# Selective-scan block: roots and fp8 casts moved to ScalarE, nine instead of six products with C of each chunk moved to GpSimd

## The chip, the cores and the metric

The kernel runs on one core of one Trainium2 chip. The metric is device time in microseconds (us), the median over runs. Engines are named as in the profile: PE is TensorE (PEld its weight loads), DVE is VectorE, ACT is ScalarE, POOL is GpSimd, SP is SyncE, which here only issues DMAs. Each engine runs its own instructions in the order in which the program wrote them; engines wait for one another through semaphores.

## The reference

The input is x of shape (8, 96, 64, 64) in float32: 8 images, 96 channels, 4096 positions. Layer 0 is a selective scan, layer 1 a linear attention and a quantised two-layer network.

```python
u = groupnorm(x) as tokens;  xm, z = u @ in_proj_w.T          # 192 channels each
xm = silu(conv1d(xm, 4 taps));  dt, Bm, Cm = xm @ x_proj_w.T   # 6, 16, 16
delta = softplus(dt @ dt_proj_w.T + dt_proj_b);  A = -exp(A_log)
h[t] = exp(delta * A) * h[t-1] + delta * Bm * xm               # 16 states per channel
y = sum over states of h * Cm, + D * xm;  y = y * silu(z)
x = x + layernorm(y @ out_proj_w.T)
t = t + attention(layernorm(t))                                # linear: (q k^T) v, no softmax
t = t + ffn(layernorm(t))       # operands rounded to fp8 (5,2), sums to fp16, relu between
```

## The kernel before

**Tiling.** Images go in pairs (p, 4 of them) and positions in chunks of T = 512 (c, 8 of them), so there are 32 chunks, worked one after another. A chunk's scan has 192 channels x 16 states x 2 images = 6144 rows. A *unit* is two tiles of 128 rows x 512 positions, and a chunk has NU = 24 units: j (3 groups of 64 channels) x g (4 groups of 4 states) x b (2 halves of the states). Unit u has j = u // 8, g = (u // 2) % 4, b = u % 2.

**A unit** (`unit`, L711) has these operations.
- `products_b` (L656): POOL multiplies du (delta times xm, spread over the states) by a row of B, which gives dbu. It runs AHEAD = 3 units early, into four buffers.
- `decay` (L675): ACT computes exp(delta A) into a PSUM tile da, once for each half h; there are two da buffers, so the decay of the next unit starts when this unit's scan of the same half has ended.
- The scan (L741): DVE computes hs from da and dbu, two instructions of 512 positions. hs has three buffers.
- The product with C: in most units PE first makes a tile cc in PSUM by a selection matmul (`rows_c`, L664), and DVE multiplies hs by cc (L763), giving pr. In the units listed in POOLED, POOL does it instead (`pooled`, L767) at the start of the next unit, from a tile c that a broadcast DMA has filled with rows of C (`rows`, L639).
- `sums` (L688): PE adds the pr tiles of a pair of units over their states into the PSUM tile y. `gate` (L707) on DVE multiplies the finished y of a group j by silu(z).
- A small copy on ACT (L719) keeps the last state of the unit for the next chunk.

**Everything else** is written as generators that are advanced between units by a table, STEPS (L37): the text before the bar is run ahead of the scans of a unit, that behind it after them. P (`chain_p`) prepares the chunk after the next: group norm, convolution, Silu, B, C, delta with Softplus. E (`chain_e`) does the output projection, layer norm and residual of the chunk before, and the norm of the attention. W builds the attention matrices of an image pair. F0 and F1 (`chain_f`) do attention and the two-layer network of a chunk that lies LAG = 9 back, one for each image; they start with chunk 9, and those of the last nine chunks make up the tail of the program. G collects group-norm statistics of the next pair.

**What sets the order.** The program is written under a manual schedule: instructions stand on each engine in program order. `later` (L381) puts a few jobs on lists that `now` empties at fixed places of a unit: "norms" at its start, "others" after its scans; `settle` empties one early if its result is needed. At unit SILU = 10 two decays of unit 12 are written early into other PSUM banks, since Silu's long block on ACT follows.

**Norms.** `norm_stats` (L399) has DVE collect mean and variance, then on POOL: minus the mean (L412), add eps (L131), the root by a power of -0.5 (L132), and the product that gives the shift (L414). `normalise` (L418) is an ACT instruction with that scale and shift. A chunk has two norms of E (8 columns) and, from chunk 9 on, two of F (4 columns).

**Casts.** In F, `rounded` copies a matmul result to fp16 on ACT (L997), `relu` applies bias and relu (on ACT in the chunks, L1007; on DVE in the tail, L1003), and a job on "others" has POOL cast it to fp8 (L1011). The second matmul (L1033) needs the three casts.

**Tables.** ACT needs an activation table for Silu, one for Softplus and one for Exp; a load (ACT_TABLE_LOAD) stands in front of the first instruction that needs a table not in place.

Of the kernel before, what the change touches and what calls it, by code (L numbers as in the profile page):

```python
# [8 lines left out]
F32 = mybir.dt.float32  # L9
F32R = mybir.dt.float32r  # L10
F16 = mybir.dt.float16
# [4 lines left out]
C = 96  # L16
NS = 16
NJ = 3
NG = 4
# [5 lines left out]
POOLED = (4, 5, 12, 13, 20, 21)  # L25
POOLED_G = 2
SILU = 10
ROWS_B = (16, 18, 20, 22)
AHEAD = 3

# [10 lines left out]
    3: "F1 F0 P | F1 G6",  # L41
    4: "| E",
# [23 lines left out]
def tile_mamba_linear_attention_ffn(  # L66
# [60 lines left out]
    nc.vector.memset(mhalf, -0.5)  # L127

# [102 lines left out]
    def passing(shape, name):  # L231
        t = p2.tile([128, 2, T], F32, tag="pr", name=name, bufs=4)
        return view(t, shape)
# [165 lines left out]
    def norm_stats(src, n, tag):  # L399

        mv = p2.tile([128, n, 2], F32, tag=f"mv{tag}", name="mv")
        rstd = p2.tile([128, n], F32, tag=f"rs{tag}", name="rs")
        nmr = p2.tile([128, n], F32, tag=f"nm{tag}", name="nm")
        st = p1.tile([128, n, 6], F32, tag=f"st{tag}", name="st")
        for i in range(n):
            nc.vector.bn_stats(st[:, i, :], src[:, i, :])  # L406
        for i in range(n):
            nc.vector.bn_aggr(mv[:, i, :], st[:, i, :])


        def ends():
            nc.gpsimd.tensor_scalar_mul(nmr, mv[:, :, 0], -1.0)  # L412
            rsqrt(rstd, mv[:, :, 1], 1e-5)
            nc.gpsimd.tensor_mul(nmr, nmr, rstd)  # L414

        return rstd, nmr, later("norms", ends)

    def normalise(dst, src, norm, q):  # L418
        settle(norm[2])
        nc.scalar.activation(  # L420
            dst, src, AF.Identity, bias=norm[1][:, q : q + 1], scale=norm[0][:, q : q + 1]
        )
# [4 lines left out]
    def load_x(p, c):  # L427

        t = p1.tile([C, 2, T + 3], F32, tag="x", name="x")
        h = 3 if c else 0  # L430
        if not c:
            nc.gpsimd.memset(t[:, :, 0:3], 0.0)
        nc.sync.dma_start(
            t[:, :, 3 - h : T + 3],
            x[2 * p : 2 * p + 2, :, c * T - h : (c + 1) * T].rearrange("b c t -> c b t"),
        )
        x_next[p, c] = t

    def chain_p(p, c, s, after):
# [53 lines left out]
        nc.scalar.activation(zs, zs, AF.Silu)  # L493
        yield
# [26 lines left out]
        nc.scalar.activation(delta, delta, AF.Softplus)  # L521
        yield
# [18 lines left out]
    def first_p(s, after):  # L541
# [75 lines left out]

        cs = s["cs"] = p2.tile([128, T], F32R, tag="cs", name="cs")
# [3 lines left out]
        rows(s, "c", 2 * NS, POOLED_G)  # L622
# [16 lines left out]
    def rows(s, to, of, g):  # L639

        t = s[to, g] = p2.tile([128, 2, T], F32, tag=to, name=to, bufs=NG if to == "b" else 1)
        for n in range(NG):
            nc.sync.dma_start(
                t[32 * n : 32 * n + 32],
                s["bd"][of : of + 2 * NS].rearrange("(b n) t -> n b t", b=2)[NG * g + n]
                .unsqueeze(0)
                .to_broadcast([32, 2, T]),
            )

    def rows_b(s, g):  # L650
        rows(s, "b", 0, g)
# [12 lines left out]
    def rows_c(s, u):  # L664
        j, g, b = where(u)
        if u in POOLED:
            return
        if ("low", 0) in s:
            settle(s["low", 0])
        cc = s["cc", u] = ps_all.tile([128, T], F32, tag="cc", name="cc", bufs=2)  # L670
        nc.tensor.matmul(  # L671
            cc, lhsT=sel[64:128, g, b], rhs=s["cs"][64:128, :], start=True, stop=True
        )
# [37 lines left out]
    def unit(s, prev, nxt, first, u, steps):  # L711
# [4 lines left out]
        if u - 1 in POOLED:  # L716
            pooled(s, u - 1)
# [10 lines left out]
        if u - 3 in POOLED and u % 2 == 0:  # L728
            sums(s, u - 3)
        if u % 2 == 0 and (u or prev is not None) and (u - 1) not in POOLED:  # L730
            sums(s if u else prev, (u or NU) - 1)
# [3 lines left out]
        if to is not None:  # L735
            products_b(to, v)
        hs = s["hs", u] = p2.tile([128, 2, T], F32, tag="hs", name="hs", bufs=3)
# [22 lines left out]
        if u in POOLED:  # L760
            return
        pr = s["pr", u] = p2.tile([128, 2, T], F32, tag="pr", name="pr", bufs=4)
# [4 lines left out]
    def pooled(s, u):  # L767
        j, g, b = where(u)
        pr = s["pr", u] = p2.tile([128, 2, T], F32, tag="pq", name="pr")
        nc.gpsimd.tensor_mul(  # L770
            pr, s["hs", u], s["c", g][:, b, :].unsqueeze(1).to_broadcast([128, 2, T])
        )
# [165 lines left out]
    def chain_f(p, c, b, banks, lane=None):  # L938
# [5 lines left out]
        def place(tag, out_tag, bufs):  # L944
# [5 lines left out]
            [128, NK, C], F32, name="x2", **place(f"x2{b}", ("pr", "b")[(lane or 0) % 2], 4)  # L950
# [34 lines left out]
        casts = []  # L985
# [13 lines left out]
        def relu(m):  # L999
# [6 lines left out]
            else:  # L1006
                nc.scalar.activation(h16[m], h16[m], AF.Relu, bias=b1q[:, m : m + 1])  # L1007
            casts.append(
                later(
                    "others",  # L1010
                    lambda: nc.gpsimd.tensor_copy(h8[0][:, m, :], h16[m], saturate=False),  # L1011
                )
            )
# [15 lines left out]
        for job in casts:  # L1029
            settle(job)  # L1030
# [6 lines left out]
        y16 = p2.tile([C, T], F16, name="y16", **place("y16", "pq", 2))  # L1037
# [73 lines left out]
    waiting.update(norms=[], others=[])  # L1111
    with tc.manual_schedule():
# [5 lines left out]
        for i, (p, c) in enumerate(chunks):  # L1118
# [4 lines left out]
            def steps(u, part):  # L1123
                if part == 0:
# [6 lines left out]
                    if nxt is not None and u == NU - 1:  # L1131
                        rows(nxt, "c", 2 * NS, POOLED_G)
# [9 lines left out]
    s = slots[N - 1]  # L1142
    sums(s, NU - 1)
# [83 lines left out]
```

## Time and profile before

| | us |
|---|---|
| median of 3 runs (3163.77 to 3164.42) | 3163.89 |
| span of the profiled execution | 3160.5 |
| first scan starts, last scan pair starts | 69.5, 3005.7 |
| busy: PE, DVE, ACT, POOL | 2469.6, 2935.2, 2263.9, 2840.7 |
| one chunk, median of the time between the first scans: chunks 0 to 8, 9 to 30 | 87.5, 93.9 |

The profile is of one execution. A row of the groups reads: line, engine, operation, output <- inputs, shapes, count | busy us, mean ns of one | idle time of the engine just before such instructions and what ended it. A row of the waits reads: who waited <- for whom: us in total, times, the longest. A row of the order of time reads: start, duration, engine, line, operation, count, and in brackets the idle time before it. A row of the stretches has, after the window and its length, the busy us and the count of instructions of each engine in it. Matmul ends are modelled, so PE's busy time is no measure of its peak. "Idle before" matters only on the engine that sets the pace.

### The profile page before, as it was taken

Reading aid. Unit: us, or ns where it says so; the run is one execution under the profiler, and the core shown is the slowest. Engines: PE = TensorE matmul, PEld = TensorE weight load, DVE = VectorE, ACT = ScalarE, POOL = GpSimd, SP = SyncE. Lnnn points to the kernel's source line nnn. Section 1 sums busy time; section 2 is a strip of 40 time slices with the busy share of each in tenths; the row PEclk is TensorE's granted clock in tenths of the full one; section 3 lists DMA queues with packets and bytes.
Section 4 is the critical chain, followed back from the end, with each engine's and each line's share of the span. In section 5 each row is a group of like instructions: output and inputs, shape, how many; then the busy total and the mean of one; then the engine's idle time right before and its main releaser. Section 6 shows DMA issues by size and latency. Waiting matters only on the chain. (4 is left out here: it accounts for less than half of the span.)

```text
span 3160.5 us, 35127 instructions
## 1 busy us (share of the span) xinstructions
PE 2469.6 (78%) x9450; PEld 928.7 (29%) x9450; DVE 2935.2 (93%) x4265; ACT 2263.9 (72%) x4360; POOL 2840.7 (90%) x1921
## 2 busy tenths in 40 slices
PE   6787787878787777777777778777888778887777
PEld 2122222222222223222233323222323222332344
DVE  4999999999999999999999999999999999999945
ACT  3666666667677777777777777777877777777656
POOL 2999999999999999999999999999999999999955
PEclk8677777787778888888888877898888888877668
DMA  6655556665555667555667555567565466755322
GB/s 149 152 122 137 134 156 152 160 150 135 141 143 135 138 162 175 146 129 125 141 164 170 141 146 125 137 157 170 146 148 127 124 144 162 169 132 134 95 70 73
DMA packets 253037, 443.75 MB, mean 140 GB/s; under 512 B 37605, under 2 KB 45990, under 8 KB 252838
## 3 DMA queue, kind: packets, MB, share of 16 engines
q1 hardware_dynamic: 247846, 439.40, 56.9%
q10 hardware_dynamic: 4992, 2.11, 0.3%
q8 instruction: 74, 1.21, 0.2%
q14 instruction: 125, 1.02, 0.1%
HBM read 349.11 MB, written 92.27 MB: 140 GB/s over the span
## 5 line engine op out<-in xcount | busy, mean ns | idle before, releaser
L659 POOL TENSOR_TENSOR dbu<-du,b 128x1024 f32<-128x1024 f32 x768 | 1804.6, 2371 | 112.6 <-DVE hs L741 65.5
L741 DVE TENSOR_TENSOR_SCAN hs<-da,state,dbu 128x512 f32<-128x512 f32 x1290 | 1573.5, 1265 | 25.6 <-ACT da L681 24.6
L681 ACT ACTIVATE da<-dl,aneg 128x512 f32<-128x512 f32 x1474 | 1000.6, 688 | 665.4 <-DVE hs L741 644.2
L763 DVE TENSOR_TENSOR pr<-hs,cc 128x1024 f32<-128x1024 f32 x576 | 698.7, 1213 | 35.1 <-DVE hs L741 0.5
L695 PE MATMUL y<-pr,ssum 128*32 128x512 f32 x2816 | 585.1, 831 | 113.3 <-DVE pr L763 113.3
L770 POOL TENSOR_TENSOR pr<-hs,c 128x1024 f32<-128x1024 f32 x192 | 453.8, 2363 | 36.6 <-DVE hs L741 30.4
L459 PE MATMUL mp<-u,wk 96*64 96x512 f32 x1488 | 398.1, 658 | 66.6 <-ACT xm L477 66.4
L671 PE MATMUL cc<-cs,sel 64*128 64x512 f32 x576 | 330.0, 583 | 144.8 <-DVE pr L763 144.4
L671 PEld LDWEIGHTS cc<-cs,sel 64*128 64x128 f32 x576 | 121.6, 215 | 557.3 <-DVE pr L763 296.8
L741 DVE TENSOR_TENSOR_SCAN hs<-da,dbu 128x512 f32<-128x512 f32 x184 | 213.2, 1205 | 17.4 <-POOL dbu L659 9.9
L516 PE MATMUL mp<-dbl,dtT 12*128 12x512 f32 x186 | 158.9, 947 | 56.8 <-ACT cs L506 38.5
L695 PEld LDWEIGHTS y<-pr,ssum 128*32 128x32 f32 x2816 | 87.9, 132 | 380.6 <-DVE pr L763 201.6
L791 PE MATMUL mE<-woT,zs 128*128 128x192 f32 x744 | 146.6, 350 | 66.7 <-ACT t1e L799 45.1
L459 PEld LDWEIGHTS mp<-u,wk 96*64 96x64 f32 x1488 | 97.0, 145 | 293.6 <-issue 156.6
L132 POOL TENSOR_TENSOR rs<-rs,mhalf 128x8 f32<-128x8 f32 (+1 forms) x128 | 173.3, 1354 | 10.7
L791 PEld LDWEIGHTS mE<-woT,zs 128*128 128x128 f32 x744 | 127.3, 200 | 126.8 <-ACT t1e L799 70.5
L703 PE MATMUL y<-xm,dd 128*128 128x512 f32 x192 | 129.2, 760 | 22.4 <-DVE zs L709 21.9
L467 PE MATMUL mp<-u,wz 96*64 96x512 f32 x372 | 137.0, 825 | 4.3 <-ACT xm L485 4.3
L1011 POOL CAST h<-h 128x512 fp8e5<-128x512 f16 x192 | 117.6, 622 | 24.8 <-DVE h L1003 15.8
L719 ACT COPY state<-hs 128x2 f32<-128x2 f32 x736 | 130.1, 181 | 0.2
L420 ACT ACTIVATE o<-x,nm,rs 128x96 f32<-128x96 f32 x256 | 98.6, 455 | 36.4 <-POOL nm L414 34.4
L531 POOL TENSOR_TENSOR du<-delta,xm 128x512 f32<-128x512 f32 x93 | 117.1, 1273 | 0.0
(306 smaller groups left out, 3234.1 us busy)
## 6 DMA issues: line engine op xcount, KB each, us to landing
du<-lu SPq DMA_DIRECT2D x380, 256.0 KB, 5.5
dl<-ld SPq DMA_DIRECT2D x380, 256.0 KB, 7.9
b<-bd SPq DMA_DIRECT2D x512, 128.0 KB, 5.0
lu<-du SPq DMA_DIRECT2D x96, 256.0 KB, 5.7
ld<-delta SPq DMA_DIRECT2D x93, 256.0 KB, 2.4
c<-bd SPq DMA_DIRECT2D x128, 128.0 KB, 4.4
xg<-in_x_dram SPq DMA_DIRECT2D x32, 384.0 KB, 3.8
xr<-in_x_dram SPq DMA_DIRECT2D x32, 384.0 KB, 8.7
```

The lines of the kernel that those rows point to most:

```text
L132: nc.gpsimd.tensor_tensor(out_, out_, mhalf[0 : out_.shape[0], 0 : out_.shape[1]], op=ALU.pow)
L459: nc.tensor.matmul(ps[64 * b : 64 * b + 64, :], lhsT=wk[:, k, 64 * j : 64 * j + 64], rhs=u[:, b, k : k + T], start=(k == 0), stop=(k == 3),)
L467: nc.tensor.matmul(ps[64 * b : 64 * b + 64, :], lhsT=wz[:, 64 * j : 64 * j + 64], rhs=u[:, b, 3 : T + 3], start=True, stop=True,)
L516: nc.tensor.matmul(ps, lhsT=dtT[:, j, :], rhs=dbl[0 : 2 * RANK, :], start=True, stop=True)
L659: nc.gpsimd.tensor_mul(dbu, s["du", j][:, 2 * b : 2 * b + 2, :], s["b", g][:, b, :].unsqueeze(1).to_broadcast([128, 2, T]),)
L671: nc.tensor.matmul(cc, lhsT=sel[64:128, g, b], rhs=s["cs"][64:128, :], start=True, stop=True)
L681: nc.scalar.activation(da, s["dl", j][:, 2 * b + h, :], AF.Exp, scale=aneg[:, 2 * j + h, g : g + 1])
L695: nc.tensor.matmul(s["y"][q : q + 32, :], lhsT=ssum, rhs=pr[:, h, :], start=False, stop=(g == NG - 1),)
L741: nc.vector.tensor_tensor_scan(hs[:, h, :], s.pop(("da", u, h)), dbu[:, h, :], 0.0 if first else state["last"][:, u, h : h + 1], ALU.mult, ...
L763: nc.vector.tensor_mul(pr, hs, s.pop(("cc", u)).unsqueeze(1).to_broadcast([128, 2, T]))
L770: nc.gpsimd.tensor_mul(pr, s["hs", u], s["c", g][:, b, :].unsqueeze(1).to_broadcast([128, 2, T]))
L791: nc.tensor.matmul(ps[:, 2 * k * C : 2 * (k + 1) * C], lhsT=zs[:, j, tok : tok + 128], rhs=woT[:, j].rearrange("p b c -> p (b c)"), start= ...
```

## The change

Six things, in one edit.
- POOLED becomes 0, 2 and 5 of every eight units (nine in a chunk instead of six), and those products are issued as before at the start of the next unit.
- Their rows of C come in three tiles of 128 x 512 (c0, c1, c2), each loaded by four broadcast DMAs, in units 20 and 22 of the chunk before and in unit 1, instead of one tile of 128 x 1024 loaded in unit 23.
- All products share one rotation of PRB = 5 buffers (before: four for DVE's and two for POOL's). The sums of the pairs (0,1) and (2,3) of eight move to units 3 and 5, those of (4,5) and (6,7) to the next unit 0.
- The root is now Ln (with eps as bias) and Exp (scale -0.5) on ACT, and a negation there; POOL keeps one product per norm, written behind `products_b` of the unit. Group norm keeps the old root.
- In the chunks, the fp8 cast runs on ACT directly behind the relu. In the tail it stays on POOL.
- After Silu and after Softplus the table with Exp and Ln is loaded explicitly. One F0 step moves from unit 3 to unit 4.

```diff
-POOLED = (4, 5, 12, 13, 20, 21)
-POOLED_G = 2
+POOLED = (0, 2, 5)
+ROWS_POOLED = {20: (0, 0), 22: (1, 0), 1: (2, 1)}
+PRB = 5
-    3: "F1 F0 P | F1 G6",
-    4: "| E",
+    3: "F1 P | F1 G6",
+    4: "| F0 E",
...
-        def ends():
-            nc.gpsimd.tensor_scalar_mul(nmr, mv[:, :, 0], -1.0)
-            rsqrt(rstd, mv[:, :, 1], 1e-5)
-            nc.gpsimd.tensor_mul(nmr, nmr, rstd)
-        return rstd, nmr, later("norms", ends)
+        def power():
+            nc.scalar.activation(rstd, mv[:, :, 1], AF.Ln, bias=eps5)
+            nc.scalar.activation(rstd, rstd, AF.Exp, scale=-0.5)
+            nc.scalar.mul(nmr, rstd, -1.0)
+        def shift():
+            nc.gpsimd.tensor_mul(nmr, nmr, mv[:, :, 0])
+        return rstd, nmr, (later("norms", power), later("shifts", shift))
...
+    def exp_and_ln():
+        nc.scalar.preload_act_table_set("natural_log_exp_and_others")
...
         nc.scalar.activation(zs, zs, AF.Silu)
+        exp_and_ln()
...
         nc.scalar.activation(delta, delta, AF.Softplus)
+        exp_and_ln()
...
+    def rows_pooled(s, g, b):
+        t = s["c", g, b] = p2.tile([128, T], F32, tag=f"c{g}", name="c", bufs=1)
+        for n in range(NG):
+            row = 2 * NS + NS * b + NG * g + n
+            nc.sync.dma_start(
+                t[32 * n : 32 * n + 32], s["bd"][row : row + 1].to_broadcast([32, T])
+            )
...
-        if u - 1 in POOLED:
+        if u and (u - 1) % 8 in POOLED:
             pooled(s, u - 1)
...
-        if u - 3 in POOLED and u % 2 == 0:
-            sums(s, u - 3)
-        if u % 2 == 0 and (u or prev is not None) and (u - 1) not in POOLED:
-            sums(s if u else prev, (u or NU) - 1)
+        if u % 8 == 0 and (u or prev is not None):
+            of, v = (s, u) if u else (prev, NU)
+            sums(of, v - 3)
+            sums(of, v - 1)
+        if u % 8 in (3, 5):
+            sums(s, u - 2)
         now("norms")
         steps(u, 0)
...
             products_b(to, v)
+        now("shifts")
...
-        pr = s["pr", u] = p2.tile([128, 2, T], F32, tag="pq", name="pr")
+        pr = s["pr", u] = p2.tile([128, 2, T], F32, tag="pr", name="pr", bufs=PRB)
...
-            casts.append(
-                later("others",
-                    lambda: nc.gpsimd.tensor_copy(h8[0][:, m, :], h16[m], saturate=False)))
+            if after:
+                nc.gpsimd.tensor_copy(h8[0][:, m, :], h16[m], saturate=False)
+            else:
+                nc.scalar.activation(h8[0][:, m, :], h16[m], AF.Copy, saturate=False)
...
-                    if nxt is not None and u == NU - 1:
-                        rows(nxt, "c", 2 * NS, POOLED_G)
+                    if u in ROWS_POOLED:
+                        to = s if u < NU // 2 else nxt
+                        if to is not None:
+                            rows_pooled(to, *ROWS_POOLED[u])
```

## The prediction

> **What bounds the kernel now.** I read the busy shares first, then the stretches of time, then the groups of instructions, then the chain of waits, and last the order of time in one chunk.
>
> ```profile
> PE 2469.6 (78%) x9450; PEld 928.7 (29%) x9450; DVE 2935.2 (93%) x4265; ACT 2263.9 (72%) x4360; POOL 2840.7 (90%) x1921
> ```
> ```profile
> core 0: us, PE busy (x) PEld busy (x) DVE busy (x) ACT busy (x) POOL busy (x), PEclk, DMA share, GB/s
> 69.00:856.00 787.00, 620.51 (x2159) 202.83 (x2159) 766.66 (x935) 526.62 (x985) 727.70 (x393) 0.76 0.60 143
> 856.00:2918.00 2062.00, 1628.77 (x6418) 609.91 (x6418) 1977.94 (x2818) 1569.59 (x3015) 1934.89 (x1277) 0.83 0.60 146
> 3005.00:3160.50 155.50, 116.46 (x518) 74.20 (x518) 80.03 (x314) 93.45 (x206) 85.52 (x164) 0.74 0.23 72
> ```
>
> The first stretch is chunks 0 to 8, the second chunks 9 to 30 (with F work), the third the tail. In the first two DVE is busy 97% and 96% of the time: DVE sets the pace, POOL is close behind (92%, 94%), ACT has room (67%, 76%). Per chunk that is 87.4 us with DVE 85.2 and POOL 80.9 in the first stretch, and 93.7 us with DVE 89.9, POOL 87.9 and ACT 71.3 in the second.
>
> ```profile
> L741 DVE TENSOR_TENSOR_SCAN hs<-da,state,dbu 128x512 f32<-128x512 f32 x1290 | 1573.5, 1265 | 25.6 <-ACT da L681 24.6
> L763 DVE TENSOR_TENSOR pr<-hs,cc 128x1024 f32<-128x1024 f32 x576 | 698.7, 1213 | 35.1 <-DVE hs L741 0.5
> L770 POOL TENSOR_TENSOR pr<-hs,c 128x1024 f32<-128x1024 f32 x192 | 453.8, 2363 | 36.6 <-DVE hs L741 30.4 <-DMA xr<-in_x_dram 3.6 <-DMA xg<-in_x_dram 1.4
> L1011 POOL CAST h<-h 128x512 fp8e5<-128x512 f16 x192 | 117.6, 622 | 24.8 <-DVE h L1003 15.8 <-ACT h L1007 2.1 <-PE cc L859 1.8
> L132 POOL TENSOR_TENSOR rs<-rs,mhalf 128x8 f32<-128x8 f32 x64 | 106.8, 1670 | 5.3
> L132 POOL TENSOR_TENSOR rs<-rs,mhalf 128x4 f32<-128x4 f32 x64 | 66.5, 1039 | 5.3
> L997 ACT CAST h<-mF 128x512 f16<-128x512 f32 x147 | 85.0, 578 | 10.2 <-POOL h L1011 6.7 <-PE mF L989 3.1
> L1007 ACT ACTIVATE h<-h,b1q 128x512 f16<-128x512 f16 x138 | 97.0, 720 | 0.0
> L719 ACT COPY state<-hs 128x2 f32<-128x2 f32 x736 | 130.1, 181 | 0.2
> ```
>
> These are the prices: a product with C costs 1.213 on DVE and 2.363 on POOL, a root 1.670 or 1.039, a cast 0.622 on POOL.
>
> ```profile
> ACT da L681 <- DVE hs L741: 644.2, 820, 4.0
> DVE hs L741 <- ACT da L681: 31.7, 43, 1.2
> ```
>
> ACT mostly waits for DVE's scans (644.2 us); DVE waits 31.7 us for ACT's decays. Where, the order of time shows: units 12 to 14 of chunk 15, DVE and then ACT.
>
> ```profile
> 1468.46 2.46 DVE L741 TENSOR_TENSOR_SCAN hs<-da,state,dbu 128x512 f32<-128x512 f32 x2 [1.00 <-ACT da L681]
> 1471.59 2.46 DVE L741 TENSOR_TENSOR_SCAN hs<-da,state,dbu 128x512 f32<-128x512 f32 x2 [0.67 <-ACT da L681]
> ```
> ```profile
> 1462.04 1.28 ACT L492 ACT_TABLE_LOAD   x1
> 1463.34 1.48 ACT L492 ACTIVATE xm<-xm 128x1536 f32<-128x1536 f32 x1
> 1464.73 1.47 ACT L493 ACTIVATE zs<-zs 128x1536 f32<-128x1536 f32 x1
> 1466.10 0.27 ACT L719 COPY state<-hs 128x2 f32<-128x2 f32 x2
> 1466.38 1.28 ACT L681 ACT_TABLE_LOAD   x1
> 1467.67 1.30 ACT L681 ACTIVATE da<-dl,aneg 128x512 f32<-128x512 f32 x2
> ```
>
> Silu's block delays the decay for unit 13 by 1.00 us, and the F copies behind it delay unit 14 by 0.67 us.
>
> **Part by part.**
>
> *Products with C.* Units 0, 2, 5 of eight instead of 4, 5, 12, 13, 20, 21: 288 on POOL instead of 192. DVE loses 96 x 1.213 = 116.4 us (3.64 per chunk), POOL gains 96 x 2.363 = 226.9 (7.09 per chunk). On DVE this lies on the path. PE drops 96 selection matmuls; PE is not on the path.
>
> *Roots.* POOL loses 128 roots with the add and the negation (L131, L412, 0.231 to 0.257 each in the groups): 64 x (1.670 + 0.248 + 0.257) + 64 x (1.039 + 0.231 + 0.255) = 236.8 us. ACT gains three small instructions per norm. The trace shows no Ln; the nearest row is the 0.181 us state copy, the far end POOL's 0.257 for 128x8: 128 x 3 x 0.181 = 70 us, at most 99. I take 70, the same engine's row. Ln now waits on ACT for DVE's statistics; behind it stand the next unit's decays, which wait for a scan that DVE runs after these statistics anyway: nothing. Without that cover it would cost 0.54 per norm. The shift stays on POOL (0.204), now behind the dbu product; in unit 17 it waits for ACT's Softplus block, by my count some 2 us, and POOL is 4 us early for the next buffer it has to free. The normalisations wait for this shift; they stand a unit later or behind the decays (F0's moved from unit 3 to 4): nothing.
>
> *Casts.* POOL loses 138 x 0.622 = 85.8 us, ACT gains 138 of 0.578 (PSUM copy) to 0.720 (relu on the same SBUF tile). I take 0.63, between two near rows: 87 us. The tail's 54 stay on POOL.
>
> *Tables.* The explicit load after Silu and after Softplus replaces the one that stood before the next Exp: the built programs have 128 loads each. The row is 1.283 us per load, and the next activation starts 0.01 us behind it. Saved: at most the 0.27 us of state copies; I take 0. [...]
>
> *Rows of C and buffers.* Per chunk twelve loads of 64 KB instead of four of 128 KB, in units 20, 22 and 1, on SP's queue. Each is needed four or five units (15 to 20 us) after it is issued; the c rows land in 4.4 us. The old tile's last reader has run three units before. SP's later entries are pushed by eight more issues (one takes 0.32 us in the order of time); the loads behind them (xr, spreads) have a unit or more: 0. Five buffers for products: each takes the place of the fifth product back, whose sum has run two units before. PE's sums of pairs with a POOL product come a unit later, two units after that product was issued; the last pair and DVE's gate stay: 0, and if POOL lagged by two units, PE would wait and the pr on DVE behind it.
>
> *What the freed time runs into.* ACT's queue gets longer in units that become shorter on DVE. I follow the timeline of chunk 15 with the new items. Unit 8: DVE now 2.43, six normalisations on ACT (2.2); decay 10 is ready just in time: no wait. Units 10 to 13: pr(10) goes, pr(12) comes back; Silu's wait of 1.00 stays. Unit 13: a cast before the decay for 14, +0.53; two more before that for 15, +0.30. Unit 18 loses its pr, and the root and two u activations (0.81) stand before decay 19: +0.80. Unit 0: a cast of unit 23 before decay 1: +0.15. Sum +1.78. Against it F's second matmul no longer waits for POOL's casts (42.6 us in the waits of PE), so y16 and res come earlier; DVE waits 27.2 us at res, 19.8 of that behind ACT, over 23 chunks; I take half, -0.45.
>
> **Sum**, against the profiled span of 3160.5:
> - Chunks 9 to 31: -3.64 + 1.78 - 0.45 = -2.31, x 23 = -53.1. POOL there goes to 87.9 + 7.09 - 2 x (2.175 + 1.525) - 6 x 0.622 = 83.9, under DVE's 86.3.
> - Chunks 0 to 8: DVE 85.2 - 3.64 = 81.5; POOL 80.9 + 7.09 - 2 x 2.175 = 83.7, now the longer one. Bounds per chunk: 83.8 (DVE with its present idle 2.3) and 87.4 (nothing won). I take 85.0, nearer to POOL's own work: -2.4 x 9 = -21.6.
> - Tail: POOL -18 x 1.525 = -27 of 85.5 us, ACT +10 on 93.5, alternating in the chain. Bounds -10 and +8; I take -2.
>
> Together -76.7: 3083.8. The median lies 3.4 above this span (3163.9): 3087.
>
> **Rivals.**
> 1. DVE keeps its pace and all of its work is won, ACT's waits being absorbed: 3163.9 - 116.4 = 3047. For: ACT's 644 us of waiting. Against: the two waits shown, in units that get casts.
> 2. POOL becomes the bound in the first nine chunks and keeps its present idle 6.5 per chunk: 90.2, +2.8 x 9 = +25; with -53 and -2: 3134. For: 83.7 over 81.5. Against: POOL's idle is waiting for scans, which come sooner.
> 3. Slower: ACT's queue sets the pace in units 8 to 18. By counts and rows ACT minus DVE work goes from 1.80 to 3.02 in unit 8, 3.43 to 5.93 in 10, 2.88 to 4.14 in 13, and -0.47 to 1.35 in 18: 6.8 us per chunk. If all of it becomes DVE's wait, -3.64 + 6.8 = +3.16, x 31: 3262. It decides from 3.64 of new waiting per chunk; I count 1.78, since a decay may run a unit late before a scan waits.
> 4. No change: new waits of just 3.64: 3164.
>
> **Chances and range.** Forecast 0.50 (own range 3058 to 3112), full gain 0.16, POOL-bound 0.12, slower 0.18, no change 0.04. A measurement of this kernel can tell some 0.2% (6 us) from no change. Faster 0.78, same 0.04, slower 0.18. The range leaves out rival 3: from 3040 (rival 1 with the tail's gain) to 3152 (rival 2 with 0.720 casts and 0.257 small operations in the waits).
>
> **What would show it.** The profile after: DVE's pr x480, busy near 2820; POOL near 2745; ACT near 2420; no pow but the four of the group norm; a cast near 0.63 on ACT; DVE's waits for da near 70 to 90 us instead of 31.7; chunks of about 91 us late and 85 early. Rival 3 shows as DVE waits for da above 140 us. The prediction is wrong if Ln or the fp8 cast is far longer than its neighbours' rows, if POOL's products lag so far that scans wait for a free hs buffer, or if PE, waiting for a POOL product, delays cc.

## The result and the profile after

The changed kernel takes 3201.68 us (median; 3189.84 to 3210.36) against 3163.85 us (3163.77 to 3164.42) beside it: ratio 1.0118, 95% interval 1.0095 to 1.014. It is slower by 38 us where 77 us less was forecast. Its profiled execution has a span of 3201.6 us, 41.1 more than before.

The busy shares and three stretches (chunks 0 to 8, 9 to 30, tail) of the changed kernel:

```profile
PE 2480.9 (77%) x9610; PEld 977.6 (31%) x9610; DVE 2860.6 (89%) x4170; ACT 2403.5 (75%) x4882; POOL 2748.6 (86%) x1495
```
```profile
core 0: us, PE busy (x) PEld busy (x) DVE busy (x) ACT busy (x) POOL busy (x), PEclk, DMA share, GB/s
69.00:889.00 820.00, 614.02 (x2240) 215.21 (x2240) 753.65 (x917) 541.34 (x1046) 767.30 (x378) 0.75 0.60 145
889.00:2973.00 2084.00, 1653.10 (x6479) 652.98 (x6477) 1913.89 (x2735) 1673.15 (x3378) 1837.21 (x948) 0.79 0.58 145
3066.00:3201.60 135.60, 108.63 (x525) 65.77 (x519) 76.47 (x314) 103.08 (x273) 48.29 (x92) 0.81 0.27 82
```

Work left DVE (2935.2 to 2860.6) and POOL (2840.7 to 2748.6) as intended, but DVE's share fell from 97% and 96% to 92% in both scan stretches: it now waits. The median chunk went from 87.5 to 89.4 us early and from 93.9 to 95.3 late. From the first scan to the start of the last pair it is +60.6 us, in the tail -19.2, ahead of the first scan -0.2.

For the +60.6, DVE's ledger in that stretch says: busy -72, idle +132. Of the busy time, products are -112, the group norm's small instructions +27, scans +10 and the rest +3, with the time in which two neighbours overlap counted once, to the earlier one. The rows of the idle time, from the groups of the changed kernel (idle time and its releasers stand behind the bar):

```profile
L764 DVE TENSOR_TENSOR_SCAN hs<-da,state,dbu 128x512 f32<-128x512 f32 x1290 | 1572.9, 1265 | 70.0 <-ACT da L701 55.6 <-POOL t1e L841 8.7 <-POOL pr L793 0.2
L786 DVE TENSOR_TENSOR pr<-hs,cc 128x1024 f32<-128x1024 f32 x480 | 582.8, 1214 | 29.8 <-PE mp L469 0.5 <-PE y L715 0.5 <-DVE hs L764 0.5
L891 DVE TENSOR_TENSOR gram<-mE,gram 97x97 f32<-97x97 f32 x54 | 13.3, 246 | 72.1 <-PE mE L882 72.1
L189 DVE SCALAR_TENSOR_TENSOR gnnmr<-gnmean,gnrstd 96x2 f32<-96x2 f32 x4 | 18.8, 4696 | 1.2 <-POOL gnrstd L135 1.2
L1034 ACT ACTIVATE h<-h 128x512 fp8e5<-128x512 f16 x138 | 86.9, 630 | 4.2
L415 ACT ACTIVATE rs<-mv,eps 128x8 f32<-128x8 f32 (+1 forms) x128 | 37.8, 295 | 24.0 <-DVE mv L411 24.0
```
```profile
ACT da L701 <- DVE hs L764: 550.1, 621, 4.8
DVE gram L891 <- PE mE L882: 72.1, 24, 3.6
PE mp L469 <- ACT u L454: 71.4, 26, 3.6
DVE hs L764 <- ACT da L701: 68.7, 87, 2.5
```

The same two instructions in the kernel before:

```profile
L868 DVE TENSOR_TENSOR gram<-mE,gram 97x97 f32<-97x97 f32 x54 | 13.1, 243 | 2.5 <-PE mE L859 2.5
L186 DVE SCALAR_TENSOR_TENSOR gnnmr<-gnmean,gnrstd 96x2 f32<-96x2 f32 x4 | 0.6, 138 | 1.2 <-POOL gnrstd L132 1.2
```

The waits for decays (68.7 us) are just under the predicted band of 70 to 90. The new item is a 0.25 us instruction, the collecting of a Gram matrix (L891), which now waits 72.1 us, 24 times for some 3 us; before, that idle time was 2.5 us. TensorE waits almost the same 71.4 us for the u activations (ACT makes u, the input of the convolution mp, from the group norm). A third oddity is L189: four instructions on 96 x 2 numbers take 18.8 us. The rest of the +132: the scans' waits +55.6 (37 of it for decays), the gate +15, the statistics of F (st) and the attention weights +15, and -22 at the residual of F (res).

**Where the Gram wait comes from.** Unit times (from first scan to first scan, mean of chunks 10 to 30) put it in unit 19: 3.98 us before, 6.56 after. TensorE in chunk 18, units 18 and 19, in order of time, before and after:

```profile
1774.85 0.50 PE L671 MATMUL cc<-cs,sel 64*128 64x512 f32 x1 [1.32 <-DVE pr L763]
1775.28 1.07 PE L695 MATMUL y<-pr,ssum 128*32 128x512 f32 x8
1776.27 1.94 PE L459 MATMUL mp<-u,wk 96*64 96x512 f32 x8
1778.14 0.93 PE L859 MATMUL mE<-t1e 128*97 128x97 f32 x8
```
```profile
1806.75 0.49 PE L691 MATMUL cc<-cs,sel 64*128 64x512 f32 x1
1810.25 4.09 PE L469 MATMUL mp<-u,wk 96*64 96x512 f32 x8 [3.01 <-ACT u L454]
1814.27 0.79 PE L691 MATMUL cc<-cs,sel 64*128 64x512 f32 x1
1814.99 1.93 PE L715 MATMUL y<-pr,ssum 128*32 128x512 f32 x8
1816.85 1.52 PE L882 MATMUL mE<-t1e 128*97 128x97 f32 x8
```

Before, the sums of units 16 and 17 (y) filled the time until the convolution (mp). In the changed kernel they stand a unit later, and TensorE is idle for 3.01 us. Behind the idle time everything is slow: the convolution 4.09 instead of 1.94, the sums 1.93 instead of 1.07, the Gram matmuls 1.52 instead of 0.93. On DVE the collecting stands in front of the scans of unit 20:

```profile
1814.14 1.22 DVE L786 TENSOR_TENSOR pr<-hs,cc 128x1024 f32<-128x1024 f32 x1
1818.41 0.26 DVE L891 TENSOR_TENSOR gram<-mE,gram 97x97 f32<-97x97 f32 x1 [3.04 <-PE mE L882]
```

The granted clock (the third number from the end) in the same place, before and then after:

```profile
core 0: us, PE busy (x) PEld busy (x) DVE busy (x) ACT busy (x) POOL busy (x), PEclk, DMA share, GB/s
1774.70:1778.40 3.70, 3.55 (x20) 1.08 (x21) 3.60 (x4) 2.60 (x6) 3.62 (x4) 1.00 1.01 352
1778.40:1782.30 3.90, 2.97 (x18) 1.21 (x18) 3.80 (x6) 3.75 (x10) 3.90 (x3) 1.00 1.07 220
```
```profile
core 0: us, PE busy (x) PEld busy (x) DVE busy (x) ACT busy (x) POOL busy (x), PEclk, DMA share, GB/s
1808.60:1811.60 3.00, 1.35 (x5) 0.55 (x7) 2.48 (x4) 2.94 (x9) 3.00 (x4) 0.95 1.05 372
1811.60:1818.60 7.00, 7.00 (x27) 2.62 (x23) 3.85 (x5) 4.08 (x11) 7.00 (x4) 0.53 1.04 220
```

**Where L189 comes from.** In chunk 14 it lasts 6.21 us, until 1402.88. DVE, then POOL:

```profile
1396.67 6.21 DVE L189 SCALAR_TENSOR_TENSOR gnnmr<-gnmean,gnrstd 96x2 f32<-96x2 f32 x1
```
```profile
1393.57 4.66 POOL L679 TENSOR_TENSOR dbu<-du,b 128x1024 f32<-128x1024 f32 x2
1398.17 2.38 POOL L793 TENSOR_TENSOR pr<-hs,c 128x1024 f32<-128x1024 f32 x1
1400.49 2.37 POOL L679 TENSOR_TENSOR dbu<-du,b 128x1024 f32<-128x1024 f32 x1
1405.33 2.35 POOL L679 TENSOR_TENSOR dbu<-du,b 128x1024 f32<-128x1024 f32 x1 [2.46 <-DVE hs L764]
```

It ends 0.02 us after the third of the POOL multiplications that run beside it, at the first gap that POOL leaves. Before, the same instruction took 0.13 us in that place. L189 has two tensors of SBUF as inputs.

### The profile page after: what moved, and what is told of

It is laid out like the page before. It is cut to its first block, busy times and chain, and to the rows that moved or that the text cites. A ratio compares the mean times of both kernels' runs of the same rounds, so it can differ in the third digit from the quotient of the medians.

```text
span 3201.6 us, 36073 instructions
## 1 busy us (share of the span) xinstructions
PE 2480.9 (77%) x9610; PEld 977.6 (31%) x9610; DVE 2860.6 (89%) x4170; ACT 2403.5 (75%) x4882; POOL 2748.6 (86%) x1495
## 3 DMA queue, kind: packets, MB, share of 16 engines
q8 instruction: 76, 1.25, 0.2%
q14 instruction: 131, 1.07, 0.1%
## 4 chain that ended last, share of the span: by engine, by line
DVE 38%; ACT 28%; PE 20%; issue 9%; DMA 3%; POOL 3%; SPq 0%; DVEq 0%; ACTq 0%; POOLq 0%
DVE hs L764 30%; ACT da L701 6%; PE mp L469 4%; ACT t1e L427 3%; DVE pr L786 3%; PE mE L814 3%; PE y L715 3%; ACT L447 2%; PE mp L527 2%; DVE st L409 1%; POOL dbu L679 1%; ACT delta L532 1%; PE mE L882 1%; PE mF L1052 1%; ACT L532 1%
## 5 line engine op out<-in xcount | busy, mean ns | idle before, releaser
L764 DVE TENSOR_TENSOR_SCAN hs<-da,state,dbu 128x512 f32<-128x512 f32 x1290 | 1572.9, 1265 | 70.0 <-ACT da L701 55.6
L793 POOL TENSOR_TENSOR pr<-hs,c 128x1024 f32<-128x1024 f32 x288 | 680.6, 2363 | 132.2 <-DVE hs L764 56.5
L786 DVE TENSOR_TENSOR pr<-hs,cc 128x1024 f32<-128x1024 f32 x480 | 582.8, 1214 | 29.8 <-PE mp L469 0.5
L469 PE MATMUL mp<-u,wk 96*64 96x512 f32 x1488 | 453.6, 705 | 110.9 <-ACT u L454 71.4
L814 PE MATMUL mE<-woT,zs 128*128 128x192 f32 x744 | 190.6, 424 | 115.0 <-ACT t1e L822 97.8
L691 PE MATMUL cc<-cs,sel 64*128 64x512 f32 x480 | 273.2, 583 | 3.2 <-DVE pr L786 3.0
L509 PE MATMUL mp<-xm,xpT 128*96 128x512 f32 x186 | 149.6, 970 | 97.9 <-DVE hs L764 91.6
L814 PEld LDWEIGHTS mE<-woT,zs 128*128 128x128 f32 x744 | 168.4, 253 | 137.6 <-ACT t1e L822 111.3
L715 PEld LDWEIGHTS y<-pr,ssum 128*32 128x32 f32 x3072 | 86.9, 128 | 230.4 <-issue 183.4
L1012 PE MATMUL mF<-qT,w1T 96*128 96x512 fp8e5 x147 | 65.3, 444 | 107.5 <-ACT h L1020 105.7
L477 PE MATMUL mp<-u,wz 96*64 96x512 f32 x372 | 104.9, 643 | 16.9 <-ACT zs L500 14.2
L509 PEld LDWEIGHTS mp<-xm,xpT 128*96 128x96 f32 x186 | 44.8, 260 | 211.4 <-issue 96.4
```

The lines of the kernel that those rows point to most:

```text
L469: nc.tensor.matmul(ps[64 * b : 64 * b + 64, :], lhsT=wk[:, k, 64 * j : 64 * j + 64], rhs=u[:, b, k : k + T], start=(k == 0), stop=(k == 3),)
L509: nc.tensor.matmul(ps[0:C, :], lhsT=xpT[:, j, :], rhs=xm[:, j, :], start=(j == 0), stop=(j == NJ - 1),)
L691: nc.tensor.matmul(cc, lhsT=sel[64:128, g, b], rhs=s["cs"][64:128, :], start=True, stop=True)
L715: nc.tensor.matmul(s["y"][q : q + 32, :], lhsT=ssum, rhs=pr[:, h, :], start=False, stop=(g == NG - 1),)
L764: nc.vector.tensor_tensor_scan(hs[:, h, :], s.pop(("da", u, h)), dbu[:, h, :], 0.0 if first else state["last"][:, u, h : h + 1], ALU.mult, ...
L786: nc.vector.tensor_mul(pr, hs, s.pop(("cc", u)).unsqueeze(1).to_broadcast([128, 2, T]))
```

## The experiments

Ratios are to the kernel before, in runs on the same chip. Differences in us are between medians, some of them of different chips; the kernel before took 3163.9 to 3170.3 beside them. Unit times are means of chunks 10 to 30 of the profiled execution.

**1. The sums of (16,17) back in unit 18.** The first suspect, alone; all else as in the changed kernel.

```diff
-        if u % 8 in (3, 5):
+        if u == 18:
+            sums(s, 17)
+        if u % 8 in (3, 5) and u != 19:
             sums(s, u - 2)
```

> The changed kernel with one difference: the sums of the pair (16,17) stand in unit 18 again instead of unit 19, so that PE does them while it waits for the u activations and not between the convolution and the Gram matmuls. Theory A (the moved sums make the Gram matmul of unit 19 late, and DVE's collect of it waits 72.1 us in all): that wait falls below 15 us, unit 19 goes from 7.0 to about 4 us, time about 60 to 75 us lower than 3202, that is 3127 to 3142. Theory B (u is late on ACT, since three norm operations and a unit without a DVE product stand in front, and the convolution on PE with it): the wait falls only by the two sums at PE's rows, some 1 to 2 us of 3 per chunk, 3140 to 3175. If PE in unit 18 had to wait for POOL's product instead, no gain: 3200.

Measured: 3145.22 us, ratio 0.9934 (0.9912 to 0.9956). One moved line turns the slower kernel into a faster one, 56 us less. The idle time at the Gram collecting (with L889, the copy that begins a matrix) falls from 75.6 us to 4.6; unit 19 takes 3.97. TensorE in chunk 18:

```profile
1777.36 1.05 PE L715 MATMUL y<-pr,ssum 128*32 128x512 f32 x4 [0.51 <-DVE pr L788]
1778.34 2.44 PE L469 MATMUL mp<-u,wk 96*64 96x512 f32 x8
1780.71 0.49 PE L691 MATMUL cc<-cs,sel 64*128 64x512 f32 x1
1781.13 0.93 PE L884 MATMUL mE<-t1e 128*97 128x97 f32 x8
```

The median is 3 us above the range expected of theory A and lies in that of theory B, but the wait has gone as A says, and not by 1 to 2 us of 3. What this run can't tell is whether the order itself or the clock made the wait: both changed.

**2. The idle time filled, the order kept.** The selection matmul of unit 19 is written seven times into the same tile; the sums stay in unit 19.

```diff
-        nc.tensor.matmul(
-            cc, lhsT=sel[64:128, g, b], rhs=s["cs"][64:128, :], start=True, stop=True
-        )
+        for _ in range(7 if u == 19 else 1):
+            nc.tensor.matmul(
+                cc, lhsT=sel[64:128, g, b], rhs=s["cs"][64:128, :], start=True, stop=True
+            )
```

> The kernel after, with one edit: the selection matmul of unit 19, issued in unit 18, is done seven times into the same tile instead of once, so that TensorE is busy in the 3.0 us in which it waits for the u activations. The sums of units 16 and 17 stay in unit 19. Theory clock (it is the lower granted clock behind the idle time that makes the convolution 4.09 us instead of 1.94 and the sums 1.93 instead of 1.07): the convolution falls to 2.0 to 2.5 us, DVE's wait for the Gram matmul falls from 72 us to under 20, and the median to 3140 to 3165 us. Theory order (the sums stand in front of the Gram matmuls, whatever the clock): the convolution may become faster, but the wait stays above 45 us, and the median at 3175 to 3205 us. Six more matmuls of 0.49 us in 32 chunks are 94 us of TensorE work; if they delay the convolution themselves, the wait grows past 72 us.

Measured: 3171.04 us, ratio 1.0013 (0.9999 to 1.0027); the Gram wait is 39.6 us. By the totals both theories miss. The chunks decide, since the filling worked in half of them: of chunks 9 to 29, eleven show an idle time of at most 1.10 us before the convolution, and in every one the granted clock stays 1.00, the convolution takes 2.64 and unit 19 3.8 to 4.3 us. (The convolution takes 1.94 at the full clock where both u are ready, as before, and 2.64 where it starts behind the first.) The other ten have 1.25 to 2.15 us of idle time, a clock of 0.50 to 0.73, a convolution of 3.9 to 4.4 and a unit 19 of 5.5 to 8.1. Chunk 11 and chunk 18, the stretch from the convolution to the Gram matmuls, and TensorE's convolution in both:

```profile
core 0: us, PE busy (x) PEld busy (x) DVE busy (x) ACT busy (x) POOL busy (x), PEclk, DMA share, GB/s
1137.25:1143.33 6.08, 6.08 (x17) 1.47 (x17) 4.49 (x4) 5.43 (x13) 6.08 (x4) 0.59 1.02 254
1804.73:1809.37 4.64, 4.64 (x24) 1.78 (x25) 4.54 (x5) 4.33 (x11) 4.64 (x4) 1.00 1.03 302
```
```profile
1137.25 4.08 PE L469 MATMUL mp<-u,wk 96*64 96x512 f32 x8 [1.59 <-ACT u L454]
1804.73 2.64 PE L469 MATMUL mp<-u,wk 96*64 96x512 f32 x8 [0.89 <-ACT u L454]
```

Same order, same work: with the clock held there is no wait for the Gram matmuls, without it there is. The convolution also starts later in the ten (by 1.0 us in the median, counted from the first scan of unit 18), which can't be the 3 us. So the order alone costs nothing: the clock has to fall. In the changed kernel itself chunk 15 says the same: its clock stayed 1.00 (after 2.39 us of idle time, an exception to any simple limit), and its unit 19 took 3.87.

But the clock alone isn't it either. In the kernel before it stood at 0.50 to 0.53 under the convolution in five chunks (13, 16, 19, 20, 28), and their unit 19 took 3.86 to 4.60. Chunk 19, PE, then DVE, then the stretch of the convolution:

```profile
1872.45 3.68 PE L459 MATMUL mp<-u,wk 96*64 96x512 f32 x8
1877.73 0.26 DVE L868 TENSOR_TENSOR gram<-mE,gram 97x97 f32<-97x97 f32 x1 [0.53 <-PE mE L859]
1872.45:1876.13 3.68, 3.68 (x13) 0.84 (x9) 3.58 (x4) 3.53 (x10) 3.68 (x4) 0.50 1.03 235
```

There the sums are done ahead of the convolution, and unit 18 still has its product on DVE. In between lie four chunks of experiment 1 (1, 4, 5 and 7), with the sums in front again but that product on POOL: at a clock of 0.50 to 0.63 their unit 19 took 4.5 to 5.5 us, against 7.3 to 7.4 in the same chunks of the changed kernel. So the 3 us need both: a clock that has fallen, and the new order, with the sums between the convolution and the Gram matmuls and a unit 18 that DVE finishes sooner. How the 56 us split between these was not measured.

**3. The shift of the group norm on POOL.** The second suspect, alone.

```diff
-        nc.vector.scalar_tensor_tensor(nmr, mean, -1.0, rstd, ALU.mult, ALU.mult)
+        nc.gpsimd.tensor_mul(nmr, mean, rstd)
+        nc.gpsimd.tensor_scalar_mul(nmr, nmr, -1.0)
```

> The changed kernel, but the shift of the group norm, one DVE instruction of 96x2 with two SBUF inputs (156 to 6225 ns in the changed kernel, 130 to 157 before), is made by two small POOL instructions. Theory L (DVE's instruction waits until POOL leaves a gap between two of its own): the three 6.2 us stretches go, 17 to 19 us less, 3183. Rival (the stretch only covers a wait for something else, ACT's Silu block that ends at the same time): DVE waits there for ACT's decay instead, under 5 us less.

Measured: 3184.19 us, ratio 1.0062 (1.0045 to 1.008): 17.5 less, about the three stretches of 6.2 us (18.6). The medians alone leave some 9 us of that open either way.

**4. The shift on DVE with one SBUF tensor.** Two instructions; rstd enters as a scalar for each partition.

```diff
-        nc.vector.scalar_tensor_tensor(nmr, mean, -1.0, rstd, ALU.mult, ALU.mult)
+        for b in range(2):
+            nc.vector.tensor_scalar(
+                nmr[:, b : b + 1], mean[:, b : b + 1], rstd[:, b : b + 1], -1.0,
+                ALU.mult, ALU.mult,
+            )
```

> The changed kernel with the group norm's shift still on DVE, as two instructions that read one SBUF tensor each and take the other factor as a per-partition scalar. If it is the second SBUF tensor that makes DVE wait for a gap of POOL, the 6.2 us stretches go and about 17 us with them: 3185. If any small SBUF instruction of DVE there waits in the same way, they stay: 3200.

Measured: 3185.44 us, ratio 1.0072 (1.0045 to 1.0098), as good as experiment 3. Same engine, same place in the order, and the stretches are gone:

```profile
L190 DVE TENSOR_SCALAR gnnmr<-gnmean,gnrstd 96x1 f32<-96x1 f32 x8 | 1.2, 196 | 1.2 <-POOL gnrstd L135 1.2
```

So with one SBUF tensor and a scalar the instruction doesn't wait for POOL's multiplications. That a second tensor is what it takes isn't shown, though. In the same chain a copy of one SBUF tensor (gnm) waits too: in the kernel before it took 2.00 us in chunk 6, until 0.02 us after a POOL multiplication, and in experiment 1, with three of them in its way:

```profile
607.47 5.79 DVE L173 COPY gnm<-gnmv 96x2 f32<-96x2 f32 x1
```

**5. Both repairs.** The edits of experiments 1 and 3 together.

> The changed kernel with just two repairs: the sums of (16,17) in unit 18, and the group norm's shift on POOL. If the two waits are independent, 56 and 17 us less than 3202: 3125 to 3132. If the freed time runs into a wait behind them, 3140 to 3150.

Measured: 3118.42 us, ratio 0.9859 (0.9838 to 0.9881). That is 83 less than the changed kernel and below both expectations. It is 10 more than 56 + 17.5, which is no more than the intervals of the four medians leave open.

**6. The ScalarE half alone.** The kernel before with roots, casts, explicit tables and the moved F0 step; products, rows, buffers and sums as before. Against the changed kernel:

```diff
-POOLED = (0, 2, 5)
-ROWS_POOLED = {20: (0, 0), 22: (1, 0), 1: (2, 1)}
+POOLED = (4, 5, 12, 13, 20, 21)
+POOLED_G = 2
...
-PRB = 5
...
-        if u % 8 == 0 and (u or prev is not None):
-            of, v = (s, u) if u else (prev, NU)
-            sums(of, v - 3)
-            sums(of, v - 1)
-        if u % 8 in (3, 5):
-            sums(s, u - 2)
+        if u - 3 in POOLED and u % 2 == 0:
+            sums(s, u - 3)
+        if u % 2 == 0 and (u or prev is not None) and (u - 1) not in POOLED:
+            sums(s if u else prev, (u or NU) - 1)
```

> The kernel before with roots, casts, explicit table loads and the F0 step moved as in the change, but with its six POOL products, its rows of C, its buffers and its sums. It prices the ACT half alone. If ACT's longer queue is what costs (rival 3 of the prediction), it is slower than before by 2 to 3 us per chunk with F: 3215 to 3235. If POOL was not the bound and ACT's room covers it: 3155 to 3175, since POOL loses 323 us that nobody waits for. The Gram wait of unit 19 should stay near the 2.5 us of before, as the sums of (16,17) stay in unit 18.

Measured: 3202.82 us, ratio 1.0123 (1.0108 to 1.0139), between the two expectations. Without fewer products on DVE, the longer ACT queue costs more than it brings: DVE's waits for decays are 56.3 us, and statistics of F (st) wait 24.1 us for F0's normalisations, now in unit 4 (unit 5 +0.5 us, unit 6 +1.0). Units 13 and 14 grow by 0.63 and 0.34, as in the forecast (+0.53, +0.30).

**7. The GpSimd half alone.** Experiment 1 with roots and casts back on POOL.

```diff
-        def power():
-            nc.scalar.activation(rstd, mv[:, :, 1], AF.Ln, bias=eps5)
-            nc.scalar.activation(rstd, rstd, AF.Exp, scale=-0.5)
-            nc.scalar.mul(nmr, rstd, -1.0)
+        def ends():
+            nc.gpsimd.tensor_scalar_mul(nmr, mv[:, :, 0], -1.0)
+            rsqrt(rstd, mv[:, :, 1], 1e-5)
+            nc.gpsimd.tensor_mul(nmr, nmr, rstd)
...
-            if after:
-                nc.gpsimd.tensor_copy(h8[0][:, m, :], h16[m], saturate=False)
-            else:
-                nc.scalar.activation(h8[0][:, m, :], h16[m], AF.Copy, saturate=False)
+            casts.append(
+                later(
+                    "others",
+                    lambda: nc.gpsimd.tensor_copy(h8[0][:, m, :], h16[m], saturate=False),
+                )
+            )
```

> The product half alone: nine products with C on POOL, their rows, buffers and sums as in the change, but with the sums of (16,17) in unit 18, and with roots and casts on POOL as before. By counts POOL then has 87.9 + 7.1 = 95 us per late chunk against 93.7 that a chunk takes. If POOL's work is what the ACT half must free, POOL sets the pace: 3200 to 3280. If the ACT half only costs and the products gain by themselves, 3090 to 3140.

Measured: 3253.64 us, ratio 1.0275 (1.0257 to 1.0292), inside the first expectation. Its page, and its two scan stretches:

```profile
PE 2530.3 (78%) x9610; PEld 969.1 (30%) x9610; DVE 2865.9 (88%) x4170; ACT 2257.1 (69%) x4360; POOL 3058.1 (94%) x2017
```
```profile
69.00:889.00 820.00, 620.44 (x2252) 218.02 (x2248) 756.39 (x917) 533.15 (x1000) 799.89 (x424) 0.74 0.60 145
889.00:3030.00 2141.00, 1710.18 (x6541) 644.49 (x6540) 1937.74 (x2765) 1567.12 (x3021) 2091.58 (x1349) 0.78 0.58 144
```

POOL is busy 98% of both stretches, DVE 92% and 91%: POOL sets the pace. Neither half pays alone (+38 and +89 us); experiment 1, which is this kernel with roots and casts on ACT, is 20 us faster than before.

**8. Only the roots back on POOL**, in the changed kernel (the first part of the diff above).

> The changed kernel with the roots back on POOL in front of the dbu product, all else as changed. Theory A: the Gram wait stays near 70 us, and the time moves little through ACT (70 to 90 us of work gone, mostly hidden) while POOL gets 237 us back and becomes the longer engine: 3200 to 3260. Theory B: u comes 0.8 us sooner in unit 18, the Gram wait falls by 0.8 x 24 = 19 us or more.

Measured: 3185.96 us, ratio 1.007 (1.0055 to 1.0085): 16 less, below the range of theory A, though POOL is busy 2979.7 us (94%). Two things pull against each other. The Gram idle time is 39.0 instead of 75.6 us, more than theory B's 19: on ACT the three root instructions (1808.72 to 1809.49 in chunk 18) stand in front of the u activations for which TensorE waits. And the tail is 151.9 instead of 135.6 us: there the roots on ACT do save 16 us.

**9. Only the casts back on POOL**, in the changed kernel (the second part of that diff).

> The changed kernel with the casts of the chunks back on POOL, all else as changed. If the casts on ACT cost what they cost in best1 (43 us), 3160. If they cost only their delays in units 13 and 14 (0.5 and 0.4 us per late chunk), 3180. If POOL is too full to take 85.8 us back, 3200 or more.

Measured: 3168.53 us, ratio 1.001 (0.9999 to 1.0021): 33 less, between the two lower expectations. DVE's waits for decays fall from 68.7 to 34.6 us, units 13 and 14 from 3.63 and 4.36 to 3.08 and 4.02. POOL, rid of the roots, has the room (89%).

**10. More sums early.** Experiment 5, with the sums of the pairs (4,5) of eight in units 7, 15 and 23, and the squared deviation of the group norm on POOL too. Against the changed kernel; the lines of the shift, as in experiment 3, are left out:

```diff
-        nc.vector.tensor_sub(dev, m0, mean)
-        nc.vector.tensor_mul(dev, dev, dev)
-        nc.vector.tensor_add(dev, dev, mv[:, :, 1])
+        nc.gpsimd.tensor_sub(dev, m0, mean)
+        nc.gpsimd.tensor_mul(dev, dev, dev)
+        nc.gpsimd.tensor_add(dev, dev, mv[:, :, 1])
...
             of, v = (s, u) if u else (prev, NU)
-            sums(of, v - 3)
             sums(of, v - 1)
-        if u % 8 in (3, 5):
+        if u == 18:
+            sums(s, 17)
+        if u % 8 in (3, 5, 7) and u != 19:
             sums(s, u - 2)
...
-    sums(s, NU - 3)
     sums(s, NU - 1)
```

> The changed kernel with the sums of (16,17) in unit 18, those of (4,5) of eight in unit 7 instead of the next unit 0, and the four small DVE instructions of the group norm with two SBUF inputs (shift, and the three of the squared deviation) on POOL. If the three causes add up (-56 for the pair, -17 for the shift, and up to -25 for the 27.9 us that DVE's gate waits for PE's sums): 3105 to 3130. If the gate waits for something else, 3125 to 3135. If the waits only change places, 3140 to 3150.

Measured: 3165.22 us, ratio 1.0 (0.9988 to 1.0011), above all three expectations and 47 worse than experiment 5. The gate's wait falls to 6.0 us, but DVE's waits for decays rise to 116.3. Unit 16 takes 6.01 instead of 5.26 and unit 18 4.32 instead of 2.85 (against experiment 1). By the order of time the sums of (12,13) stand on TensorE in unit 15 in front of F's second matmul; what follows it on ACT, up to Softplus and the decays behind, comes late. Experiment 12 comes back to that reading.

**11. The same with casts on POOL.** Experiment 10 with the second part of the diff of experiment 7.

> The kernel best1 with the casts back on POOL in the chunks. ACT loses 87 us, POOL gets 85.8. If the casts on ACT delay the decays in units 13 and 14 (0.5 and 0.4 us of the prediction, seen as unit times 3.63 and 4.36 us instead of 3.11 and 3.98), up to 25 us less than best1; if POOL, with 87.6 us of work in a chunk of 91, is too full, as much or more.

Measured: 3121.87 us, ratio 0.9864 (0.9847 to 0.988): 43 less than experiment 10, where up to 25 was expected of the casts' delays. DVE's waits for decays fall from 116.3 to 77.9 us.

**12. The sums of (4,5) and (12,13) back in the next unit 0 of eight**, only (20,21) in unit 23; the rest as in experiment 11, against which the edit is shown.

```diff
+            if u:
+                sums(of, v - 3)
             sums(of, v - 1)
-        if u % 8 in (3, 5, 7) and u != 19:
+        if (u % 8 in (3, 5) and u != 19) or u == 23:
             sums(s, u - 2)
```

> The kernel best1_casts with the sums of (4,5) of eight back in the next unit 0, but for the last pair of that kind, (20,21), which stays in unit 23. In best1 the pair (12,13) in unit 15 stands on PE in front of F's second matmul, which makes y16, the third delta matmul and Softplus late: unit 16 takes 6.01 us and unit 18 4.32 us instead of 5.26 and 2.85. If that is the cause, both come back and the time falls from 3122 by 1.5 to 2.3 us per late chunk, less up to 0.3 for the gate of unit 17: 3075 to 3095. If not, 3115 to 3125.

Measured: 3094.47 us (3090.72 to 3098.97), ratio 0.9773 (0.9759 to 0.9788), better than both kernels and inside the range expected of the reading in experiment 10. Unit 16 takes 5.31 us and unit 18 2.75, as in experiment 1; but the edit moved the sums of (4,5) back as well, so it isn't a test of (12,13) by itself. Its page:

```profile
PE 2433.8 (79%) x9610; PEld 941.4 (30%) x9610; DVE 2837.5 (92%) x4154; ACT 2321.8 (75%) x4744; POOL 2825.6 (91%) x1653
```

It keeps what paid (products with C and roots) and undoes what did not (the casts, the place of the sums of (16,17) and (20,21), and the two-tensor instructions of the group norm on DVE).

## Why the prediction was wrong

**The step that failed** is in the part on rows of C and buffers: "PE's sums of pairs with a POOL product come a unit later ...: 0", together with "PE is not on the path" in the first part. I priced the moved sums by what waits for them (the gate), and not by what stood behind and around them on TensorE. In unit 18 they were the work that kept TensorE busy; without them it idles some 3 us (3.01 in chunk 18), its clock falls (to a mean of 0.53 in the 7 us behind), and the sums then stand, at that clock, in front of the Gram matmuls. DVE, whose next scans stand behind the collecting of the Gram matrix, waits. Price: 56 us (experiment 1). It takes the fallen clock (experiment 2) and the new order together (the kernel before has the low clock in five chunks, and waits 2.5 us in all). The 96 selection matmuls less I counted as relief only.

How much idle time it takes for the clock to fall, the runs don't settle: in experiment 2 its mean is 0.50 to 0.73 behind 1.25 us and more, and in the changed kernel it is once still 1.00 behind 2.39 (chunk 15). In the traces of both kernels the clock is recorded as 1.00 or 0.50 alone, in stretches of 3.41 us or whole multiples of it (but for the last one of a trace). In chunk 18 of the changed kernel, for one, it is 1.00 from 1804.47 to 1811.30 and 0.50 from there to 1818.12; the values between are means. Why it stayed up in chunk 15 was not shown.

**A term that was missing:** the group norm's DVE instructions, which the diff doesn't touch. POOL's multiplications now follow one another where L189 is issued. It cost some 17 us (experiments 3 and 4). Each of the three long L189 lasted some 6.2 us, until 0.02 us after the third of three multiplications of 2.35 to 2.38 us that ran beside it.

Without these two (experiment 5) the kernel takes 3118 us: above the forecast of 3087 and my own range, inside the stated range of 3040 to 3152.

**Point by point.**
- *Products:* 96 fewer on DVE, 582.8 instead of 698.7 us: right (-116). It was won on DVE's busy time, and lost again in its idle time.
- *Roots:* 128 table loads as before, none of them in a norm: right. Ln takes 0.295, Exp and the negation 0.207, so some 91 us instead of 70, inside the bound of 99. "Nothing" for their place was wrong in unit 18, where they delay the u activations (experiment 8).
- *Casts:* 0.630 each, 86.9 us: right in price. Their effect in the queue was foreseen (0.53, 0.30 and 0.15 per chunk, 23 us), but not that taking them back would save 33 (experiment 9).
- *ACT's queue:* +1.78 in each late chunk. DVE's waits for decays went from 31.7 to 68.7 us, just under the band I gave, and that close by luck: 17.2 of these 37 us lie in chunks 0 to 8, where I had counted none. In the late ones it is 0.86 per chunk.
- *res:* -0.45 per chunk foreseen, 10 us; the idle time fell by 22.
- *Chunks 0 to 8:* -2.4 foreseen, from a mean of 87.4; the mean measured is 90.0, +2.6. Without TensorE's wait (experiment 1) it is 88.4, and with both repairs (experiment 5) 87.4, my bound "nothing won": 2.1 of the 3.64 went to waits for decays alone (23.4 us there in experiment 1, 4.7 before).
- *Tail:* -2 foreseen from bounds of -10 and +8, -19 measured. The bounds were too narrow: the norms lie in the chain there, and on ACT the three root instructions need 0.71 us, where POOL needed 1.5 or more (experiment 8 gives the roots 16 of the 19).
- *Rivals:* POOL as the bound is what happens without the ACT half (experiment 7), not in the kernel itself (86% busy). Its 90.2 us for chunks 0 to 8 is near the 90.0 measured, but by luck: DVE waits there 25.7 us for the Gram matmuls and 21.9 for decays, and 15.1 for POOL's products, of which 9.9 stood there before. ACT's queue as the bound had its mark at waits above 140 us; 68.7 is on the other side. The slower result came by a way listed only in the last sentence, "if PE ... delays cc", and there with another cause: TensorE waited for ACT, not for a POOL product.

## What to carry to other kernels

A matmul that moves off a place may have been what keeps TensorE's clock up there: before moving it, look in the order of time for what TensorE does in the time that becomes free (here it idled 3.01 us, and the convolution behind took 4.09 us instead of 1.94), and for what stands behind it on the engine that sets the pace. When multiplications move to GpSimd, look for small VectorE instructions on SBUF tensors that now meet an unbroken row of them (here one of two tensors took 6.2 us instead of 0.13). A change of several parts is best judged by taking parts back one at a time: here two of its parts paid, a third cost 33 us, and one line of the order cost 56.

## What the runs showed of the hardware

- The traces of both kernels record the clock as 1.00 or 0.50 alone, in stretches of 3.41 us or whole multiples of it, but for the last one of each. In the 21 chunks 9 to 29 of experiment 2 its mean under the next matmuls was 0.50 to 0.73 behind idle times of 1.25 us and more and 1.00 behind at most 1.10. No limit follows from that: in the kernel before it was 0.50 under the convolution in chunks 13, 16 and 19, with 0.92 us of idle time in the 3.5 us ahead of it, and 1.00 in chunk 15 with 1.49; in the changed kernel it was 0.58 behind idle times of 1.49 and 1.21 us (chunk 17) and 1.00 behind one of 2.39 (chunk 15).
- A convolution of eight matmuls with both inputs ready took 1.94 us at the full clock and 3.68 at 0.50 (kernel before). One that starts behind the first input took 2.64 at the full clock, and 3.9 to 4.4 where the mean clock was 0.50 to 0.67 (experiment 2).
- A DVE instruction on 96 x 2 numbers with two SBUF tensors lasted 6.2 us, to the end of three POOL multiplications of 2.4 us that followed one another without a gap; with one SBUF tensor and a scalar for each partition it took 0.196 us in the same place. A copy of one such tensor lasted 2.00 us (kernel before) and 5.79 (experiment 1), each until 0.02 us after a POOL multiplication. Not every POOL instruction does this: in chunk 22 of the kernel before, three two-tensor DVE instructions took 0.16 us each inside a POOL power of 1.67 us.
- Ln and Exp followed one another on ACT in 128 norms with no table load between them (0.295 and 0.207 us for 128 x 8 or 128 x 4 numbers).
